# Four layers on one core: edge fills, a later large fill, paired Gelus and convolution rows loaded ahead

## The chip, the cores and the metric

The kernel runs on one core of a Trainium2 chip. The metric is the device time of one execution in microseconds (us). The core's engines work in parallel, each through its own instruction queue in order: PE (matmul), DVE or VectorE (elementwise and scans), ACT (activations), POOL or GpSimd (elementwise and transfers), SP (transfers alone).

## The reference, cut to what matters

The input x has 8 images of 384 channels and 32 x 32 pixels, in fp32. Four layers follow each other:

- Layer 0 normalizes x over the channels, multiplies by in_proj to get u and z, runs a four-tap convolution over the 1024 pixels in both directions, makes delta, B and C from it, and then a state scan: `h = exp(delta * A) * h + delta * u * B`, `y = sum over 16 states of h * C`, forwards and backwards. y times silu(z) goes through out_proj; a 3x3 depthwise convolution of the normalized image with a sigmoid is added.
- Layer 1: a 1x1 convolution (c1), a 3x3 depthwise convolution (dw), a 1x1 convolution (c2), linear attention, a layer norm and an MLP of 384 x 1536 x 384 with Gelu, with residual sums.
- Layer 2: seven depthwise convolutions of up to 13 x 13, summed; the kernel merges them into one 13x13.
- Layer 3: a 1x1 convolution, another 13x13 depthwise convolution, and Gelu.

## The kernel before, in words

The 384 channels are three chunks of 128 partitions, an image is two halves of 512 pixels. A scheduler of the tile framework sets the order on each engine from the order in which the program emits work; the order quoted in this text is that of the built program.

**Start.** The images with a border of zeros for the 3x3 convolutions (`xn_d`, `h_d`) and the padded sequence (`u_d`) lie in DRAM, two slots each. L464 to L470 fill all of them with zeros, in pieces of 384 elements per channel. `front(0)` (L599) then runs alone: the mean square through `rsqrt_mean` (L577: sums by PE, Ln and Exp on ACT, spreading by PE), the image stored by `put_image` (L554), the products of in_proj, the 3x3 convolution (`conv3`, L559, tiles lc_i and lc), the four-tap convolution (ut), deltas.

**Scan.** `scan(b)` (L720) has 48 rounds per image. In each, ACT makes da (L807, Exp), VectorE du (L812) and two pairs of scans hs (L824), POOL multiplies hs by C (L833, tile bct), and PE adds the states into acc (`sums`, L757, through `together`, L521). hs has eight buffers, two per round. Loads of dlt, vr and bct come through SP's queue. At the end of an image half zr (L780) is stored to `g_d`.

**Work beside the scan.** A planner at L1114 holds jobs: a generator, a planned cost, a first and a last round. After each round it advances the job that is furthest behind, by the cost that each `yield` reports. `front(b)` of the next image has a plan of 100, `layer1` of the image before one of 310, `fold` (which scales weights, and at L860 fills `x2_d`, the padded input of the 13x13 convolution, with zeros in three transfers of 5008 KB) one of 30. The layer 1 of the last image runs alone after the scans.

`layer1` (L901) multiplies g by out_proj (op, L914, added by VectorE at L916), runs c1 for half 1, then half 0, with one image store per half (L926), then dw (L933, copied by ACT at L934), c2 (L942), attention, the layer norm, and the MLP (L1072): for each of 12 groups of 128 hidden units, and each half, the first product mf, Gelu (L1081), and the second product mo (L1083). ACT loads another function table whenever it goes from exponentials to Gelu and back. PE's result tiles for most products are `psum` (tag mm, two buffers) and `long_psum` (tag mo, three).

**13x13 convolutions.** `conv` (L275) goes over 48 blocks of 8 channels. POOL loads a block's rows (xt, L290, four buffers), VectorE shifts copies of them (L296), SP and ACT load windows of taps (tp), PE multiplies (L308). `put2` stores through POOL; `put3` (L374) applies Gelu on ACT into ot (three buffers) and stores through POOL (L377).

Of the kernel before, what the change touches and what calls it, by code (L numbers as in the profile page):

```python
# [19 lines left out]
H = 32  # L20
# [48 lines left out]
def tile_layers(  # L69
# [190 lines left out]
    with tc.tile_pool(name="cw", bufs=1, reuse_waits="tile") as cwp, tc.tile_pool(  # L260
# [14 lines left out]
        def conv(g_d, src_d, tag, put):  # L275

            xt = tp = None
            for g in range(NQ):  # L280
                n, first = divmod(4 * g, NCH)
                if first == 0:
                    xt = cxp.tile([P, NCH, RL], FP, tag="xt", name=f"xt_{tag}_{n}", bufs=4)

                    at = [H * ((n % 2 * 2 + e) % NSH) for e in range(NSH)]
                    src = bass.AP(
                        src_d.tensor, src_d[NCH * n, 0, 0].offset,
                        [[RL, H], [H * RL, NCH], [1, RL]],
                    )
                    nc.gpsimd.dma_start(xt[at[0] : at[0] + H], src)  # L290
                    for m in range(n, min(n + 1 + N_WIN // 2, NB_C)):
                        if (tag, m) not in wins:
                            load_windows(g_d, tag, m, [nc.sync, nc.scalar])
                    tp = wins[tag, n]
                    for e in (1, 2):
                        nc.vector.tensor_copy(  # L296
                            xt[at[e] : at[e] + e * H, :, 0 : RL - e - (e - 1)],
                            xt[at[0] : at[0] + e * H, :, e : RL - (e - 1)],
                        )
                ps = cps.tile([P, HALF], FP, tag="cv", name=f"cv_{tag}_{g}")  # L300
                for t in range(KT):
                    for e in range(4):
                        c = first + e
                        row = xt[:, c, NSH * t : NSH * t + B * (W + PADW) - PADW]
                        rhs = bass.AP(
                            row.tensor, row.offset, [row.ap[0], [W + PADW, B], [1, W]]
                        )
                        nc.tensor.matmul(  # L308
                            ps[H * e : H * (e + 1), 0:BW],
                            tp[:, c, :].rearrange("p (j t) -> p j t", t=KT)[:, :, t], rhs,  # L310
                            start=(t == 0), stop=(t == KT - 1), skip_group_check=True,
                        )
                put(g, ps[:, 0:BW])
# [60 lines left out]
        def put3(g, ps):  # L374
            ot = cxp.tile([P, BW], FP, tag="ot", name=f"ot_{g}", bufs=3)
            nc.scalar.activation(ot, ps, AF.Gelu, bias=gbias[:, g : g + 1])  # L376
            nc.gpsimd.dma_start(  # L377
                ov[g * P : (g + 1) * P], ot.rearrange("p (b w) -> p b w", w=W)
            )
# [4 lines left out]
def _layers01(tc, nc, B, xv, x2_d, dram, ident, mean_w, eps5, eps6, one, half, minus1, vec, bns, bnt,  # L384
# [12 lines left out]
    with ExitStack() as ctx:  # L397
# [66 lines left out]
        for i in range(2):  # L464
            for t, n in ((xn_d, IMG), (u_d, UL), (h_d, IMG)):
                pads = t[i].rearrange("(c p) i -> p c i", p=P)
                for c in range(NC):
                    for a in range(0, n, C):
                        e = min(n, a + C)
                        nc.gpsimd.dma_start(pads[:, c, a:e], zero[:, 0 : e - a])  # L470
# [4 lines left out]
        def psum(name):  # L475
            return psp.tile([P, HALF], FP, tag="mm", name=name, bufs=2)
# [25 lines left out]
        def defer(n, fn):  # L502
            late.append([n, fn])
# [8 lines left out]
        def dense(ps, w, m, rhs):  # L512
            for k in range(NC):
                nc.tensor.matmul(  # L514
                    ps, w[:, k, m * P : (m + 1) * P], rhs[k] if isinstance(rhs, list) else rhs[:, k, :],
                    start=(k == 0), stop=(k == NC - 1),
                )

# [35 lines left out]
        def put_image(t_d, slot, h, t, queue):  # L554

            v = t_d[slot].rearrange("(c p) i -> p c i", p=P)
            queue.dma_start(v[:, :, (W + 2) + HIMG * h : (W + 2) + HIMG * (h + 1)], t)

        def conv3(t_d, slot, h, c, taps, name, psum=psum):  # L559

            ims, made = [], []
            for j in range(4):
                im = sp.tile([P, 18 * (W + 2)], FP, tag="im", name=f"{name}_i{j}", bufs=N_IM)
                src = bass.AP(
                    t_d.tensor, t_d[slot, 32 * (4 * c + j), 16 * h * (W + 2)].offset,
                    [[IMG, 32], [1, 3], [1, 18 * (W + 2) - 2]],
                )
                made.append(nc.sync.dma_start(im[:96, 0 : 18 * (W + 2) - 2], src))
                ims.append(im.rearrange("p (h w) -> p h w", w=W + 2))
            ps = psum(name)  # L570
            col32(
                ps, lambda j, i: taps[:96, (4 * c + j) * 3 + i, :],
                lambda j, i: ims[j][:96, i : i + 16, 0:W], 3, made,
            )
            return ps

        def rsqrt_mean(srcs, eps, name):  # L577
# [10 lines left out]
            nc.scalar.activation(r, r, AF.Exp, scale=-0.5)  # L588
            ps = psum(f"{name}_b")
# [9 lines left out]
        def front(b):  # L599

            xn = []
            for h in range(2):
# [7 lines left out]
                rstd = rsqrt_mean(sqs, eps6, f"ms_{b}_{h}")  # L610
# [7 lines left out]
                yield 3  # L618
# [18 lines left out]
            for h in range(2):  # L637
                for c in range(NC):
                    xr = t2(f"xr_{b}_{h}_{c}")
                    nc.sync.dma_start(xr, xv[b][:, c, bass.ts(h, HALF)])  # L640
                    ps = conv3(xn_d, b % 2, h, c, t3, f"lc_{b}_{h}_{c}")
# [14 lines left out]
            for h in range(2):  # L656
# [37 lines left out]
                for c in range(NC):  # L694
# [23 lines left out]
                    yield 3  # L718

        def scan(b):  # L720
# [65 lines left out]
            for k, (d, h, c) in enumerate(units):  # L786
                cols = bass.ts(h, HALF)
                second = k % (2 * NC) >= NC
                for r in range(NR):
# [12 lines left out]
                    for i in range(2):  # L802
# [32 lines left out]
                        ))  # L835
                        hs.append(t)
# [19 lines left out]
        def fold():  # L856

            RL = x2_d.shape[2]
            for c in range(NC):
                nc.gpsimd.dma_start(  # L860
                    x2v[c], zero[:, 0:RL].rearrange("p (o r) -> p o r", o=1).to_broadcast([P, H, RL])
                )
                yield 0
# [37 lines left out]
        def layer1(b):  # L901
# [17 lines left out]
            for h in (1, 0):  # L919
                hh, mid = image6(f"hh_{b}_{h}")  # L920
                for m in range(NC):
                    ps = long_psum(f"h_{b}_{m}_{h}")
                    dense(ps, w, m, xx[h])
                    nc.scalar.activation(mid[m], rows(ps), AF.Identity, bias=bias1[:, m, :])  # L924
                    yield 3
                put_image(h_d, b % 2, h, hh, nc.scalar)  # L926
            t3 = tapw(taps3b, f"t3b_{b}")
            dws = []
            for h in range(2):
                dw = a6(f"dw_{b}_{h}")  # L930
                dws.append(dw)
                for c in range(NC):
                    ps = conv3(h_d, b % 2, h, c, t3, f"dw_{b}_{h}_{c}", long_psum)  # L933
                    nc.scalar.copy(dw[:, c, :], ps)  # L934
                    yield 3
# [126 lines left out]
            for h in range(2):  # L1062
                xn = xns[h]
                sqs = [t2(f"vs_{b}_{h}_{k}") for k in range(NC)]
                for k in range(NC):
                    nc.scalar.activation(sqs[k], xn[:, k, :], AF.Square)
                rstd = rsqrt_mean(sqs, eps5, f"var_{b}_{h}")
                for k in range(NC):
                    nc.vector.tensor_mul(xn[:, k, :], xn[:, k, :], rstd)
                yield 3  # L1070

            for h in range(2):  # L1072
                acc = [long_psum(f"mo_{b}_{h}_{m}") for m in range(NC)]
                for i in range(FF // C):
                    wa = wtile(w1_d[:, i * C : (i + 1) * C], f"w1_{b}_{h}_{i}")
                    wb = wtile(w2[i * C : (i + 1) * C, :], f"w2_{b}_{h}_{i}")
                    for f in range(NC):
                        ps = psum(f"mf_{b}_{h}_{i}_{f}")
                        dense(ps, wa, f, xns[h])
                        hm = t2(f"hm_{b}_{h}_{i}_{f}")  # L1080
                        nc.scalar.activation(hm, ps, AF.Gelu, bias=biasf[:, NC * i + f, :])  # L1081
                        for m in range(NC):
                            nc.tensor.matmul(  # L1083
                                acc[m], wb[:, f, m * P : (m + 1) * P], hm,
                                start=(i == 0 and f == 0), stop=(i == FF // C - 1 and f == NC - 1),
                            )
                        yield 6

                def last(h=h, acc=acc):
                    for m in range(NC):  # L1090
                        o = xx[h][:, m, :]
                        nc.vector.scalar_tensor_tensor(  # L1092
                            o, acc[m], vec("mlp_b2", m), o, ALU.add, ALU.add
                        )
                        nc.gpsimd.dma_start(  # L1095
                            x2v[
                                m, :, h * (H // 2) : (h + 1) * (H // 2),
                                PADW + b * (W + PADW) : PADW + b * (W + PADW) + W,
                            ],
                            rows(o),  # L1100
                        )

                defer(0, last)
                yield 0
# [9 lines left out]
        jobs = [[fold(), 30, 0, rounds, 0], [prepare, 7, rounds, 2 * rounds, 0]]  # L1114
# [124 lines left out]
```

## Time and profile before

| | us |
|---|---|
| three runs, lowest / median / highest | 5220.93 / 5224.48 / 5226.53 |
| profiled execution, its own time | 5218.79 |
| span of that execution in the profile | 5217.0 |
| PE, VectorE, ACT, POOL busy | 4288.4, 3813.8, 2740.1, 2988.6 |
| first scan of image 0 starts, last pair of scans of image 7 starts | 216.9, 4187.9 |
| 13x13 convolutions, about | 4603 to 4822, 4958 to 5217 |

A window line gives, for a stretch, the busy time of each engine with its number of instructions, then the TensorE clock that was granted (1 is full speed), the busy share of the 16 DMA engines and what they moved in GB/s. A group line has the source line, engine, operation, result and operands, the count, then busy time and the mean of one in ns, and after the second bar the idle time of the engine before it and what ended it. A wait line reads "engine tile line <- what ended the wait: us in total, times, longest". PEld is PE's weight load.

### The profile page before, as it was taken

To read this page: it belongs to the slowest core of one execution; us is meant where nothing else is said; L and a number is where in the kernel's file an instruction comes from. 1 tells how busy PE (TensorE), PEld (TensorE's weight loads), DVE (VectorE), ACT (ScalarE), POOL (GpSimd) and SP (SyncE) were. 2 spreads that over 40 slices of the span, in tenths; PEclk is the share of its full clock that TensorE was granted. 3 is DMA by queue.
4 is the path that set the end of the run, shared out by engine and by line. 5 is a ranking of instruction groups with operands and counts; after the bars stand their busy time and mean duration, and the time that the engine had idled before them with its cause. 6 is when DMAs were issued, how large, how long until landed. Compare 5 with 4: busy or idle time off the path is not lost. (4 is left out here: it accounts for less than half of the span.)

```text
span 5217.0 us, 58464 instructions
## 1 busy us (share of the span) xinstructions
PE 4288.4 (82%) x20128; PEld 1783.5 (34%) x20128; DVE 3813.8 (73%) x3861; ACT 2740.1 (53%) x3816; POOL 2988.6 (57%) x1600
## 2 busy tenths in 40 slices
PE   4675568888988998899889888998878869968977
PEld 1121123333333333333333333333323324457456
DVE  0399899988888798879887888788978911056255
ACT  1455444785478557855775577567735712100211
POOL 3276666676667666766676657566856850033056
PEclk8676679899989998999899989999989989989989
DMA  9856447575756675767576757765653572289696
GB/s 285 243 200 213 160 150 224 194 211 171 211 202 196 180 218 181 208 177 223 172 221 182 220 177 201 202 214 168 176 166 121 158 157 67 61 181 251 204 192 139
DMA packets 545969, 975.11 MB, mean 187 GB/s; under 512 B 57049, under 2 KB 221385, under 8 KB 545673
## 3 DMA queue, kind: packets, MB, share of 16 engines
q1 hardware_dynamic: 401648, 663.89, 42.4%
q0 software_dynamic: 61408, 215.60, 16.1%
q10 hardware_dynamic: 82616, 91.90, 6.2%
q8 instruction: 159, 2.61, 0.2%
q14 instruction: 138, 1.12, 0.1%
HBM read 726.36 MB, written 244.81 MB: 186 GB/s over the span
## 5 line engine op out<-in xcount | busy, mean ns | idle before, releaser
L833 POOL TENSOR_TENSOR hs<-hs,bct 128x1024 f32<-128x1024 f32 x768 | 2411.2, 3140 | 991.2 <-DVE carry L829 473.1
L807 ACT ACTIVATE da<-dlt,neg_a 128x512 f32<-128x512 f32 x1536 | 1035.4, 715 | 774.4 <-DVE hs L824 721.2
L824 DVE TENSOR_TENSOR_SCAN hs<-da,du 128x512 f32<-128x512 f32 x768 | 902.2, 1208 | 243.0 <-ACT da L807 143.2
L812 DVE TENSOR_TENSOR du<-vr,bct 128x1024 f32<-128x1024 f32 x768 | 1059.3, 1379 | 25.4 <-DMA vr<-v_d 14.9
L824 DVE TENSOR_TENSOR_SCAN hs<-da,carry,du 128x512 f32<-128x512 f32 x768 | 944.0, 1267 | 56.9 <-PE acc L531 16.9
L531 PE MATMUL acc<-hs,selt 128*32 128x512 f32 x2304 | 560.8, 661 | 181.3 <-POOL hs L833 181.2
L1083 PE MATMUL mo<-hm,w 128*128 128x512 f32 x1152 | 572.9, 638 | 91.7 <-ACT hm L1081 91.4
L514 PE MATMUL mf<-ln,w 128*128 128x512 f32 x1152 | 564.4, 626 | 10.9 <-DMA w<-w_d 10.9
L526 PE MATMUL acc<-hs,selt 128*32 128x512 f32 x768 | 421.4, 647 | 75.6 <-POOL hs L833 50.4
L1083 PEld LDWEIGHTS mo<-hm,w 128*128 128x128 f32 x1152 | 219.6, 200 | 440.4 <-issue 243.7
L807 ACT ACT_TABLE_LOAD x278 | 356.7, 1283 | 7.5 <-ACT hh L924 2.7
L514 PEld LDWEIGHTS mf<-ln,w 128*128 128x128 f32 x1152 | 222.0, 200 | 334.7 <-issue 309.4
L514 PE MATMUL in<-xn,win 128*128 128x512 f32 x576 | 293.9, 642 | 13.2 <-ACT uz L628 8.8
L308 PE MATMUL cv_b<-xt_b,tp_b 128*32 128x256 f32 x3072 | 192.8, 404 | 68.2 <-DVE xt_b L296 36.6
L308 PE MATMUL cv_a<-xt_a,tp_a 128*32 128x256 f32 x3072 | 184.7, 390 | 55.5 <-DVE xt_a L296 31.0
L296 DVE COPY xt_b<-xt_b 32x2496 f32<-32x2496 f32 x96 | 146.0, 1521 | 109.4 <-DMA xt_b<-xp_d 103.1
L1081 ACT ACTIVATE hm<-mf,biasf 128x512 f32<-128x512 f32 x192 | 131.9, 687 | 176.2 <-PE mf L514 174.3
L1095 POOL DMA_DIRECT2D x_d<-xx x48 | 56.4, 1178 | 292.8 <-DVE xx L1092 292.7
L531 PE MATMUL dw<-dw_i,t3b 96*32 96x512 f32 x1056 | 210.3, 636 | 7.5 <-DMA dw_i<-h_d 7.2
L308 PEld LDWEIGHTS cv_b<-xt_b,tp_b 128*32 128x32 f32 x3072 | 160.4, 140 | 100.9 <-issue 74.1
L531 PEld LDWEIGHTS acc<-hs,selt 128*32 128x32 f32 x2304 | 93.0, 114 | 291.3 <-POOL hs L833 271.1
L1081 ACT ACT_TABLE_LOAD x146 | 187.3, 1283 | 2.6
(195 smaller groups left out, 5804.0 us busy)
## 6 DMA issues: line engine op xcount, KB each, us to landing
dlt<-dl_d SPq DMA_DIRECT2D x384, 256.0 KB, 4.2
vr<-v_d SPq DMA_DIRECT2D x384, 256.0 KB, 5.0
bct<-bc_d SPq DMA_DIRECT2D x256, 256.0 KB, 3.8
ut<-u_d SPq DMA_DIRECT2D x192, 257.5 KB, 5.6
lc_i<-xn_d SPq DMA_DIRECT2D x192, 228.8 KB, 5.4
dw_i<-h_d SPq DMA_DIRECT2D x192, 228.8 KB, 4.5
w<-w_d SPq DMA_DIRECT2D x64, 576.0 KB, 6.2
w<-in_w SPq DMA_DIRECT2D x64, 576.0 KB, 5.5
```

Of the source, the lines that this page charges most:

```text
L296: nc.vector.tensor_copy(xt[at[e] : at[e] + e * H, :, 0 : RL - e - (e - 1)], xt[at[0] : at[0] + e * H, :, e : RL - (e - 1)],)
L308: nc.tensor.matmul(ps[H * e : H * (e + 1), 0:BW], tp[:, c, :].rearrange("p (j t) -> p j t", t=KT)[:, :, t], rhs, start=(t == 0), stop=(t = ...
L514: nc.tensor.matmul(ps, w[:, k, m * P : (m + 1) * P], rhs[k] if isinstance(rhs, list) else rhs[:, k, :], start=(k == 0), stop=(k == NC - 1),)
L526: first = product()
L531: tc.keep_in_program_order(product())
L807: nc.scalar.activation(da[:, bass.ts(j, HALF)], dlt[:, bass.ts(j, HALF)], AF.Exp, scale=neg_a[:, g, r : r + 1],)
L812: nc.vector.tensor_mul(pairs(du), pairs(vt), bct[r][:, 0:1, :].to_broadcast([P, 2, HALF]),)
L824: nc.vector.tensor_tensor_scan(t[:, s][:, way], da[:, s][:, way], du[:, s][:, way], k_c if second else 0.0, ALU.mult, ALU.add,)
L833: made.append(nc.gpsimd.tensor_mul(pairs(t), pairs(t), bct[r][:, 1:2, :].to_broadcast([P, 2, HALF])))
L1081: nc.scalar.activation(hm, ps, AF.Gelu, bias=biasf[:, NC * i + f, :])
L1083: nc.tensor.matmul(acc[m], wb[:, f, m * P : (m + 1) * P], hm, start=(i == 0 and f == 0), stop=(i == FF // C - 1 and f == NC - 1),)
L1095: nc.gpsimd.dma_start(x2v[m, :, h * (H // 2) : (h + 1) * (H // 2), PADW + b * (W + PADW) : PADW + b * (W + PADW) + W,], rows(o),)
```

## The change

- The fills of `xn_d`, `u_d` and `h_d` cover only the first and the last elements (34 or 3 per channel), in 12 transfers; the inside is written by the image stores anyway.
- The three fills of `x2_d` in `fold` depend on the newest multiplication of POOL, report a cost of 2 each, and `fold` has a plan of 36.
- In `layer1`, c1 runs in an order that finishes chunks 0 and 1 first, each chunk is stored by itself, and the rows of a 3x3 convolution are loaded one convolution ahead (`rows3`, split from `conv3`); dw runs chunk by chunk.
- `rsqrt_mean` ends after Ln and Exp; the spreading is a function of its own, with a `yield` between.
- In the MLP, Gelus come as two together and one alone; the second products of a group are emitted after the next group's first products and Gelus, at a cost of 7 per group.
- In `conv`, loads of rows are emitted two blocks ahead, shifts one block ahead, windows before rows; ot has six buffers.

```diff
@@ conv
+            def load(n):
+                for m in range(n, min(n + 1 + N_WIN // 2, NB_C)):
+                    if (tag, m) not in wins:
+                        load_windows(g_d, tag, m, [nc.sync, nc.scalar])
...
+                nc.gpsimd.dma_start(xt[at[0] : at[0] + H], src)
+            for n in range(2):
+                load(n)
+            shift(0)
...
-                    nc.gpsimd.dma_start(xt[at[0] : at[0] + H], src)
+                    load(n + 2)
+                    if n + 1 < NB_C:
+                        shift(n + 1)
@@ put3
-            ot = cxp.tile([P, BW], FP, tag="ot", name=f"ot_{g}", bufs=3)
+            ot = cxp.tile([P, BW], FP, tag="ot", name=f"ot_{g}", bufs=6)
@@ fills
-        for i in range(2):
-            for t, n in ((xn_d, IMG), (u_d, UL), (h_d, IMG)):
+        for t, n, e in ((xn_d, IMG, W + 2), (u_d, UL, 3), (h_d, IMG, W + 2)):
+            for i in range(2):
                 pads = t[i].rearrange("(c p) i -> p c i", p=P)
-                for c in range(NC):
-                    for a in range(0, n, C):
-                        e = min(n, a + C)
-                        nc.gpsimd.dma_start(pads[:, c, a:e], zero[:, 0 : e - a])
+                for a in (0, n - e):
+                    nc.gpsimd.dma_start(
+                        pads[:, :, a : a + e],
+                        zero[:, 0 : NC * e].rearrange("p (c e) -> p c e", e=e),
+                    )
@@ fold
+                tc.add_manual_dep(fill.ins, newest[0].ins.name, behind, reason="fill")
+                yield 2
@@ front
-                rstd = rsqrt_mean(sqs, eps6, f"ms_{b}_{h}")
+                yield 0
+                r = rsqrt_mean(sqs, eps6, f"ms_{b}_{h}")
+                yield 1
+                rstd = spread_rows(r, f"ms_{b}_{h}")
@@ layer1, c1 and dw
-            for h in (1, 0):
-                hh, mid = image6(f"hh_{b}_{h}")
-                for m in range(NC):
...
-                put_image(h_d, b % 2, h, hh, nc.scalar)
+            for m, h in ((0, 1), (1, 1), (0, 0), (1, 0), (2, 1), (2, 0)):
+                if (m, h) == (2, 0):
+                    ahead = ready()
...
+                put_image(h_d, b % 2, h, hhs[h][0], nc.scalar, slice(m, m + 1))
+            while ahead:
+                c, h, loaded = ahead
+                ahead = ready() if todo else None
+                ps = conv3(loaded, c, t3, f"dw_{b}_{h}_{c}", long_psum)
@@ layer1, MLP
-                    for f in range(NC):
-                        ps = psum(f"mf_{b}_{h}_{i}_{f}")
-                        dense(ps, wa, f, xns[h])
...
-                        yield 6
+                    for fs in [(0, 1), (2,)]:
...
+                        together([
+                            partial(nc.scalar.activation, hm, ps, AF.Gelu, bias=biasf[:, NC * i + f, :])
+                            for f, hm, ps in zip(fs, hms, pss)
+                        ], [made])
+                        if behind_gelu:
+                            behind_gelu.pop()()
...
+                        behind_gelu.append(second)
+                        yield 7
@@ planner
-        jobs = [[fold(), 30, 0, rounds, 0], [prepare, 7, rounds, 2 * rounds, 0]]
+        jobs = [[fold(), 36, 0, rounds, 0], [prepare, 7, rounds, 2 * rounds, 0]]
```

## The prediction

> **What bounds the kernel now.** The page's chain of waits names only the last 8% of the span, so I cut the span into its stages and read the busy time of each engine in them. The boundaries are the first and last scan instruction of VectorE (L824), found in its groups of instructions, and the first and last matmul of each 13x13 convolution.
>
> ```profile
> core 0: us, PE busy (x) PEld busy (x) DVE busy (x) ACT busy (x) POOL busy (x), PEclk, DMA share, GB/s
> 0.00:216.00 216.00, 113.74 (x399) 35.76 (x400) 23.41 (x75) 44.38 (x62) 56.42 (x109) 0.77 0.96 277
> 216.00:715.00 499.00, 314.49 (x1085) 96.67 (x1081) 454.55 (x430) 273.18 (x380) 327.72 (x160) 0.71 0.55 186
> 715.00:3747.00 3032.00, 2657.39 (x9994) 992.77 (x9992) 2577.70 (x2583) 2005.79 (x2721) 1988.84 (x891) 0.93 0.65 196
> 3747.00:4195.00 448.00, 370.76 (x1263) 144.82 (x1262) 382.39 (x386) 247.68 (x353) 317.45 (x113) 0.90 0.50 145
> 4195.00:4603.00 408.00, 326.72 (x950) 137.69 (x952) 36.43 (x51) 68.40 (x110) 64.84 (x101) 0.90 0.46 94
> 4603.00:4822.00 219.00, 186.59 (x3090) 159.97 (x3086) 156.85 (x148) 17.86 (x48) 70.02 (x68) 0.98 1.06 239
> 4958.00:5217.00 259.00, 192.77 (x3072) 160.44 (x3072) 145.98 (x96) 45.49 (x96) 151.02 (x144) 0.93 0.79 166
> ```
>
> The start (0 to 216) is bound by transfers: the DMA share is 0.96 while no engine is half busy, but PE. Image 0 (216 to 715) runs at VectorE's pace, 455 of 499 us. Images 1 to 6 (715 to 3747) have VectorE 85% busy: 3032 - 2578 = 454 us of idle time, 76 per image. Image 7 idles 66 us more. The tail (4195 to 4603) is PE alone. The first 13x13 convolution has the DMA engines full; the second has 259 - 193 = 66 us without a matmul.
>
> What ends VectorE's idle time in images 1 to 6:
>
> ```profile
> DVE hs L824 <- ACT da L807: 133.8, 49, 10.6
> DVE hs L824 <- PE acc L531: 68.4, 25, 5.6
> DVE xx L916 <- PE op L514: 58.3, 26, 4.4
> DVE qp L1043 <- PE rzb L1042: 25.2, 20, 3.9
> DVE lg L646 <- ACT lg L643: 25.0, 23, 1.9
> DVE xx L942 <- PE c L514: 23.9, 11, 4.1
> DVE ln L1069 <- PE var_b L591: 14.0, 12, 2.5
> ```
>
> These are late arrivals in queues that run in order. VectorE waits for exponentials stuck on ACT behind a Gelu or a convolution's copy, and for hs buffers that PE has not yet summed because other products stand before the sums.
>
> **What the Trainium skill says.** "ScalarE: Activation LUTs", What ACT_TABLE_LOAD costs: about 1283 ns a load and a drain of about 1380 ns. The trace agrees on the first and shows no such drain (at 14.16 us a load starts 0.02 us after the activation before it), so I count 1283:
>
> ```profile
> L807 ACT ACT_TABLE_LOAD x278 | 356.7, 1283 | 7.5 <-ACT hh L924 2.7
> L1081 ACT ACT_TABLE_LOAD x146 | 187.3, 1283 | 2.6
> ```
>
> "DMA: Bandwidth & Descriptors", Queues, rings and completion order: each DMA engine goes round robin between its queues by packets, so a large fill slows the loads of other queues. The trace agrees: lc_i loads land in a median 15.9 us during the start and 5.4 over the kernel. Same page, Specifications: below 512 B a write is read-modify-write; the new edge fills have pieces of 136 and 12 B. The nearest row, the old 2 KB remainders of xn_d, lands in 4.9 us. "SBUF — State Buffer", SBUF: two separate sides: a fp32 VectorE copy keeps GpSimd from writing descriptors. The trace agrees: L377 takes 1146 ns beside the copies L296, the similar store L712 563 ns in the scan.
>
> **The change, part by part.**
>
> *Zero-fills (L470, L860).* Gone from the start are 66 small fills, 2 x 384 x (1156 + 1030 + 1156) x 4 B = 10.3 MB, and three large ones, 15.4 MB, that move behind the first scan rounds; 12 edge fills come, 0.2 MB. 25.7 MB at the 277 GB/s of the stage are 93 us, the ceiling. By events:
>
> ```profile
> DVE lg L646 <- ACT lg L643: 120.7, 6, 82.5
> PE lc L526 <- DMA lc_i<-xn_d: 48.5, 3, 38.6
> SPq L568 <- DMA xn_d<-xn: 24.3, 1, 24.3
> ```
>
> Now image 0's second half lands at 27.0 (issued 11.4), its products run from 33.9 to 66.4, lc from 105 to 163, the four-tap conv of the first half to 184, the scan begins at 216. Without fills the second half lands near 17 (5.6 us, like other 768 KB loads), so the products end near 57. The image is stored at about 28 and in the rows' order of SP eight lc loads now stand before the weights that wait for a buffer, so lc starts at 57. Six chunks at 5.5 us (half of a landing of 5.4, plus 2.6 us on PE, rounded up) end near 90, three more near 106; the unchanged 31 us of deltas and loads follow: scan at 137, **80 us** earlier. Bounds 50 and 93.
>
> The large fills are now issued after the multiplications of rounds 0, 2 and 5 of the built order. 15.4 MB take 15.4/277 = 56 us of the engines where their share is 0.55 to 0.75, so most fits into the free part. POOL reuses eight completion counters in turn: the eighth transfer after the first fill, a store of v, waits for its landing (31.5 us), and behind it on POOL stand the next multiplications L833, for which PE's sums wait. VectorE has eight hs buffers, four rounds of 7.8 us = 31 us, to go on. I charge **10 us**; bounds 0 and 35.
>
> *Convolution rows, c1 order, image store in chunks (L554, L559, L918 to L935).* In the before, all rows wait for a store of 816 KB (8.3 us) and their load (4.5) with ACT's copies dw (L934) in order before the exponentials. Image 3 shows a 9.6 us stop of VectorE there and 4.1 us at L942. Counted in the built order (a 128x512 product is two instructions of 0.43 us, as they follow each other in the start), PE's work between two sums falls there from 26 us to 8. Gain per image: 10 of 13.7.
>
> *Products in pairs, second product one step later (L1072 on).* Gelu groups fall from 24 to 16 an image; in the built program ACT's table loads fall from 653 to 572: 81 x 1.283 = 104 us of ACT. ACT is 66% busy, so this lies beside VectorE's work and counts only through the waits on da: 14.2 us of image 3 fall in the Gelu stretch, I take half, 7. PE no longer waits for Gelu (91.7 us, L1083 in the groups).
>
> *Costs of a step.* Layer 1's steps sum to 322 against a plan of 310 before, and to 290 after. So before, the rest of an image's MLP runs into the next image: PE has 38 us of products between two sums at the boundary, 18 after. Image 3 stops there for 7.6 us on sums and, with g loaded only after SP was free at 1750, 12.5 us on op (L916), 3 more after it: 23. The chain sum, store, load, product stays, so I leave 8: gain 15. Against it, the first MLP rounds have 34 us between two sums where before the largest was 21: up to 34 - 21 = 13 us of stop, charged 6.
>
> *Split means (L577).* var_b 2.4 and ms_b 2.4 per image: gain 3. rzb, lg, pj, zr (11.7 per image) stay.
>
> Per image 10 + 7 + 15 - 6 + 3 = 29, of 76 idle. Queues give late arrivals back elsewhere; I take 25 (bounds 8 and 36), for six images **150 us**. Image 7: op 18.7 and c 16.4 us of waits on VectorE, **25 us** (5 to 35).
>
> *Tail.* The last MLP of image 6 leaves the tail: the last sum waits on PE until 4214 although POOL's product ended at 4193, g is loaded at 4243. At 4194 the same 12 us of store and load give 4208: 35 us. dw waits 20 us (L526) between the last h product and its rows; a chunked store and one load, 13 us, started 7.7 us earlier leave 6: gain 13. Half of the former may be work already counted in image 7, so **35 us** (15 to 50). Its MLP has no PE gap over 0.9 us: nothing.
>
> *13x13 convolutions.* "Two blocks ahead" moves little: in the built order of before, POOL already issues each row load two or three blocks ahead. The 13.9 us at its start wait for xp_d and stay. Six ot buffers remove ACT's waits for the store, 41.7 us of ACT, of which 11.6 reach PE: **10 us** (-5 to 25).
>
> Sum: 80 - 10 + 150 + 25 + 35 + 10 = 290. The profiled execution took 5218.8 (span 5217.0); 5218.8 - 290 = 4929. Since the median of the runs is 5.7 above it and bounds lie lower on the gain side, I say **4940**.
>
> **Rivals.** *A, the forecast* (0.72): 4850 to 5030. *B, the scan gives its gains back* (0.21): the MLP is packed into 17 of 48 rounds with 8 to 9 us of PE each beside sums of about 1, against VectorE's 7.8; PE becomes the bound there and only start, tail and convolutions remain: 5224 - 70 - 35 - 10 = 5109, or about 5080 with a fifth of the scan's gain. For it: PE is 88% busy. Against it: that counts overlapping pieces; PE has rounds without any product after. *C, slower* (0.05): a pair holds both PSUM buffers "mm" until both Gelus are done. A Gelu group takes 1.28 + 2 x 0.69 us behind up to four exponentials of 0.715, 5.5 us, covered by the previous group's products, 2.6 us after a single. If PE, with the sums queued behind, stops VectorE 3 us in each of 16 steps of 7 images, 336 us are lost: 5270. It decides from 290 / 112 = 2.6 us a step. Against it: hs buffers absorb single stops. *D* (0.02): no effect beyond 0.2%, about what a measurement of this kernel tells from no change.
>
> **How the numbers follow.** A and B are faster, C slower. 4850 to 5100 takes in A and most of B. Faster 0.93, same 0.02, slower 0.05.
>
> **What would show it.** First scan at 125 to 150 us; VectorE idle under 60 us an image; no MLP product after the last scan; table loads x572; dw rows wait under 8 us; out waits on ACT near zero. An unchanged image period (505 us) would prove B; PE waits "mf <- ACT hm" of hundreds of us, C. A scan start after 180 would break the first step.

## The result and the profile after

The changed kernel takes 5048.59 us (5042.81 to 5056.85); the kernel before took 5225.5 us in the same set of runs. The ratio is 0.9663 (95% interval 0.9646 to 0.9680), 177 us or 3.4% faster. The prediction said 4940 us, so the direction and the range (4850 to 5100) held, and the size was too large: 285 us were forecast.

The view by stages of the changed kernel, cut where the same events fall (first scan of image 0, of image 1, of image 7, last scan, first and last product of each 13x13 convolution):

```profile
core 0: us, PE busy (x) PEld busy (x) DVE busy (x) ACT busy (x) POOL busy (x), PEclk, DMA share, GB/s
0.00:142.00 142.00, 98.66 (x404) 34.43 (x406) 23.99 (x75) 45.54 (x64) 25.19 (x52) 0.89 0.88 246
142.00:672.00 530.00, 296.62 (x1056) 93.02 (x1054) 457.45 (x432) 265.78 (x373) 330.31 (x163) 0.68 0.63 203
672.00:3638.00 2966.00, 2635.57 (x10080) 1003.75 (x10080) 2556.48 (x2589) 1923.45 (x2662) 2005.15 (x893) 0.94 0.67 202
3638.00:4066.00 428.00, 365.87 (x1266) 145.99 (x1268) 377.77 (x383) 231.79 (x339) 313.28 (x111) 0.92 0.53 153
4066.00:4433.00 367.00, 302.10 (x878) 129.67 (x874) 32.42 (x46) 64.93 (x106) 65.09 (x99) 0.88 0.45 96
4433.00:4645.00 212.00, 185.52 (x3070) 159.70 (x3072) 155.88 (x143) 17.51 (x47) 66.09 (x68) 0.98 1.07 244
4795.00:5048.00 253.00, 193.57 (x3072) 163.79 (x3072) 144.94 (x94) 45.49 (x96) 154.84 (x140) 0.94 0.79 165
```

Against the same events of before (216.9, 718.2, 3747.9, 4190.4, 4602.8 and the end at 5217.0):

| stage | before | after | gained | forecast |
|---|---|---|---|---|
| start, to the first scan | 216.9 | 142.4 | 74.5 | 80 |
| image 0 | 501.3 | 529.5 | -28.2 | -10 |
| images 1 to 6 | 3029.7 | 2966.0 | 63.7 | 150 |
| image 7 | 442.5 | 428.5 | 14.0 | 25 |
| tail | 412.4 | 366.8 | 45.6 | 35 |
| 13x13 convolutions, pointwise between | 614.2 | 614.8 | -0.6 | 10 |
| sum | 5217.0 | 5048.0 | 169.0 | 290 |

The size of the start came near the forecast. Of the 121 us that are missing, 86 lie in images 1 to 6. VectorE's waits there (ms_b and var_b are the spread mean squares of the front's norm and of layer 1's, rzb the spread reciprocals of the attention, lg the sigmoid branch of the 3x3 convolution, zr the gated output):

```profile
DVE hs L857 <- PE acc L551: 165.7, 57, 11.7
DVE qp L1087 <- PE rzb L1086: 27.8, 18, 4.4
DVE xn L644 <- PE ms_b L619: 27.7, 10, 4.5
DVE lg L677 <- ACT lg L674: 25.8, 24, 3.0
DVE xx L952 <- PE op L533: 22.5, 7, 6.3
DVE hs L857 <- ACT da L840: 12.4, 13, 1.5
```

The waits that the change was to remove are gone or shorter: da fell from 133.8 us to 12.4, op from 58.3 to 22.5, and c (23.9) left the list. In their place the waits for hs buffers that PE has not summed yet rose from 68.4 us to 165.7, with stops of up to 11.7, and ms_b from 5.4 to 27.7. I then sorted VectorE's idle gaps over 0.3 us of the six images by round (48 to an image; a round begins with every second product du, L845). Per image, in us:

| rounds | before | after | what it was, and what it is |
|---|---|---|---|
| 0 to 7 | 17.4 | 4.5 | op and sums at the boundary; op |
| 8 to 12 | 13.1 | 8.3 | da behind dw, c2; sums |
| 13 to 29 | 15.3 | 15.4 | rzb, lg, var_b; the same |
| 30 to 38 | 14.7 | 9.0 | da in the Gelu stretch; sums, dl |
| 39 to 47 | 3.0 | 18.9 | sums, ms_b; sums (round 46 has 9.3), ms_b |

The first, second and fourth line give 23.4 us an image; the last takes 16 back. What is left is 7 us, and 3 more in smaller gaps and busy time, together the 10.6 us an image of the stage table. So the question for the runs was whether the crowded end of the image is a fault beside the gains or their price.

### The profile page after: what moved, and what is told of

Same layout as the page of the kernel before. It is cut to its first block, busy times and chain, and to the rows that moved or that the text cites. A ratio compares the mean times of both kernels' runs of the same rounds, so it can differ in the third digit from the quotient of the medians.

```text
span 5048.0 us, 58439 instructions
## 1 busy us (share of the span) xinstructions
PE 4205.7 (83%) x20128; PEld 1787.7 (35%) x20128; DVE 3789.3 (75%) x3861; ACT 2632.2 (52%) x3735; POOL 2975.1 (59%) x1546
## 3 DMA queue, kind: packets, MB, share of 16 engines
q0 software_dynamic: 58048, 205.76, 15.4%
## 5 line engine op out<-in xcount | busy, mean ns | idle before, releaser
L845 DVE TENSOR_TENSOR du<-vr,bct 128x1024 f32<-128x1024 f32 x768 | 1019.2, 1327 | 46.3 <-DMA vr<-v_d 34.9
L533 PE MATMUL mf<-ln,w 128*128 128x512 f32 x1152 | 546.1, 620 | 22.8 <-DMA w<-w_d 11.7
L1166 PE MATMUL mo<-hm,w 128*128 128x512 f32 x1152 | 530.3, 599 | 13.8 <-DVE xx L1133 13.8
L546 PE MATMUL acc<-hs,selt 128*32 128x512 f32 x768 | 428.5, 653 | 74.4 <-POOL hs L866 63.7
L840 ACT ACT_TABLE_LOAD x233 | 298.9, 1283 | 9.5 <-DMA dw_i<-h_d 3.0
L326 PE MATMUL cv_b<-xt_b,tp_b 128*32 128x256 f32 x3072 | 193.6, 407 | 67.9 <-DVE xt_b L302 44.1
L533 PE MATMUL op<-g,wo 128*128 128x512 f32 x288 | 156.4, 695 | 61.3 <-DMA g<-g_d 61.3
L533 PEld LDWEIGHTS in<-xn,win 128*128 128x128 f32 x576 | 114.1, 207 | 215.2 <-issue 161.5
L326 PEld LDWEIGHTS cv_a<-xt_a,tp_a 128*32 128x32 f32 x3072 | 159.7, 138 | 74.3 <-issue 28.7
```

What stands on the lines that cost most here:

```text
L326: nc.tensor.matmul(ps[H * e : H * (e + 1), 0:BW], tp[:, c, :].rearrange("p (j t) -> p j t", t=KT)[:, :, t], rhs, start=(t == 0), stop=(t = ...
L533: product = nc.tensor.matmul(ps, w[:, k, m * P : (m + 1) * P], rhs[k] if isinstance(rhs, list) else rhs[:, k, :], start=(k == 0), stop=(k ...
L546: first = product()
L840: nc.scalar.activation(da[:, bass.ts(j, HALF)], dlt[:, bass.ts(j, HALF)], AF.Exp, scale=neg_a[:, g, r : r + 1],)
L845: nc.vector.tensor_mul(pairs(du), pairs(vt), bct[r][:, 0:1, :].to_broadcast([P, 2, HALF]),)
L1166: nc.tensor.matmul(acc[m], wb[:, f, m * P : (m + 1) * P], hm, start=(i == 0 and f == 0), stop=(i == FF // C - 1 and f == NC - 1),)
```

## The experiments

The kernels ran in three sets on three chips, on which the kernel before took 5270, 5227 and 5236 us. The first set holds e1 to e4, the second c1 and e5 to e7, the third e8 to e11 (the numbers are only names). So kernels of different sets are compared by their ratio to the kernel before on the same chip; a hundredth of that ratio is 52 us. The changed kernel is at 0.966; of the three sets it ran in the second alone. Kernels of one set are also compared by stages; where stages of different sets stand side by side, the text says so.

**Its own time again (c1).**

> The changed kernel itself, unaltered, beside the kernel before on this chip. Both theories: 0.9663 of the kernel before, as measured first; it is the base for the others.

5051.61 us, ratio 0.9656 (0.9634 to 0.9677). Its start (142.0) and tail (367.0) agree with the first profile; image 0 took 521.2 us instead of 529.5 and images 1 to 6 2976.6 instead of 2966.0, which shows how far the stages of one kernel differ.

**The start (e2, e1).** Large fill first again, plan 30:

```
-                fill = nc.gpsimd.dma_start(...)
-                tc.add_manual_dep(fill.ins, newest[0].ins.name, behind, reason="fill")
-                yield 2
+                nc.gpsimd.dma_start(...)
+                yield 0
```

> The changed kernel with the three large fills back at the start and their plan of 30, the edges alone otherwise. Theory 1 (15.4 MB at 277 GB/s are 56 us of a stage that is bound by transfers): first scan near 190 us, image 0 in about 501 us, so 5049 + 48 - 28 = 5069 us. Rival (the start has room for them beside its computing, because its products, not its transfers, set it now): first scan below 160 us, image 0 in about 501 us, 5030 us or less, faster than the changed kernel.

5168.51 us, ratio 0.9811 (0.9790 to 0.9832). And with the small fills over whole buffers as well:

> The changed kernel with all zero-fills as before: small fills over the whole buffers and the three large ones, all at the start. Theory 1 (the two stages pay for themselves: 74.5 us won at the start, 28 us lost in image 0, nothing carried on): first scan near 217 us, image 0 in about 501 us, 5049 + 46 = 5095 us (5085 to 5105). Rival (the start's gain was given back later, in a place not seen): within 10 us of 5049.

5190.29 us, ratio 0.9842 (0.9824 to 0.9860). The first scan came at 207.4 us with the large fill first and at 226.4 with all fills, against 144.3 in the kernel with single products (below), which has the changed start and ran on the same chip; image 0 took 508.9, 508.2 and 532.3 us. So there the small fills are worth 18 us up to image 1 and the large one 40: 63 us earlier, 23 lost in image 0. Both rivals fall. The ratios say more than theory 1, 96 us for the whole part where 46 were expected; 58 us of it stand in these two stages. The rest sits in images 1 to 7, the tail and the convolutions, where this part does nothing and where this chip made the kernel before slower too; the changed kernel wasn't run on it, so this rest stays open. Another order is not the reason as far as image 3 shows: there ACT, VectorE, POOL and SP run the same instructions in the same order as in the changed kernel.

These two kernels show that the moved fill costs image 0 some 23 us. Where it costs them can be looked for in the waits of POOL and VectorE, here in the changed kernel between 142 and 672 us, the last line in the kernel before between 217 and 718:

```profile
POOL v_d L744 <- DMA x_d<-zero: 14.1, 1, 14.1
```

```profile
DVE du L845 <- DMA vr<-v_d: 23.9, 3, 18.4
DVE hs L857 <- ACT da L840: 18.8, 6, 6.6
DVE zr L813 <- PE acc L551: 13.1, 4, 4.2
DVE hs L824 <- ACT da L807: 10.3, 4, 5.4
```

The first fill is issued at 154.9 and lands at 181.7. POOL's fourth store of v after it waits 14.1 us for that, as the prediction said. Other transfers pay too: VectorE waited 10.3 us for da in image 0 before and 18.8 now, and for vr loads, which were no wait before, 5.5 us besides the 18.4 that end where the first scan begins. Together these are 14 of the 28 us by which image 0 grew. Not all of the rest is the fill's: zr's wait for sums rose from 6.8 to 13.1, and it is 15.0 with the large fill first as well.

**Layer 1's rows (e5).** Image store in one piece, rows asked for where they are used:

```
+            for h in (1, 0):
+                hh, mid = image6(f"hh_{b}_{h}")
+                ...
+                put_image(h_d, b % 2, h, hh, nc.scalar)
...
-                ahead = ready() if todo else None
-                ps = conv3(loaded, c, t3, f"dw_{b}_{h}_{c}", long_psum)
+                ps = conv3(rows3(...), c, t3, f"dw_{b}_{h}_{c}", long_psum)
```

> The changed kernel with the image store in one piece, the h order and the 3x3 rows of layer 1 as before. Theory 1 (the traces before and after: VectorE's stops in rounds 8 to 12 fell from 13 us an image to 8, and the tail's 13 us): 5 x 6 + 13 = 43 us slower than the changed kernel. Rival (the part is worth the 10 us an image of the forecast): 60 + 13 = 73 us slower. Second rival (what it saves at round 9 comes back at once): within 10 us of it.

5137.37 us, ratio 0.9816 (0.9793 to 0.9839). Images 1 to 6 took 3038.0 us, 61.4 more than the changed kernel's 2976.6 in this set, or 10.2 an image; the tail 374.1 against 367.0. The rival, the forecast's 10 us an image, is right for these images; theory 1's 5, read off the gaps of the two traces, was half of it. The tail lost 7, where both had said 13. Its waits of VectorE in images 1 to 6:

```profile
DVE hs L857 <- PE acc L551: 128.4, 40, 11.9
DVE hs L857 <- ACT da L840: 85.5, 26, 12.1
```

The da wait of round 9 is back, 9.0 us an image.

**Pairs (e3).** The hidden products one at a time, the second product still one step later:

```
-                    for fs in [(0, 1), (2,)]:
+                    for fs in [(0,), (1,), (2,)]:
...
-                        yield 7
+                        yield 4 if fs[-1] == 2 else 5
```

> The changed kernel with the hidden products one at a time instead of in pairs, still with the second product one step later; costs 5, 5, 4 in place of 7, 7 per three, so the plan's total stays 290. Theory 1 (pairs help ACT: fewer table loads, fewer late exponentials): table loads rise from 572 towards 650, VectorE's waits for da return by some 5 us an image, 5049 + 35 = 5084 us. Rival (a pair makes a lump of products that stops the sums): waits of hs for acc fall by 8 us an image in the last 16 rounds, 4995 us.

5177.65 us, ratio 0.9828 (0.9807 to 0.9849). Images 1 to 6 took 3058.4 us against 3006.1 with the large fill first on the same chip, which has the pairs: 8.7 us an image. The forecast had 7. Table loads are 649, as theory 1 expected. Its rival is right about the sums, since the stops of rounds 39 to 47 fall from 21.8 us an image to 6.8, but not about the time: more comes back in other rounds. The waits, images 1 to 6:

```profile
DVE hs L857 <- ACT da L840: 129.7, 80, 4.2
DVE hs L857 <- PE acc L551: 111.7, 35, 8.9
DVE xx L952 <- PE op L533: 63.6, 10, 12.6
```

But this run does not show that the table loads are the cause. Although its costs sum to 290 as well, the last hidden products still run in round 0 of the next image (seen at image 3), where those of the changed kernel end in round 46, and op stops VectorE for 10.6 us an image where it was 7.8 with the pairs. And with cost 9 (below) the pairs stay, with 573 table loads, and VectorE waits for da just as long (129.1 us). So the 8.7 us are what this edit costs in this arrangement.

**The planner's costs (e4, then e8 to e10).** First, layer 1 as a whole at the pace of before:

```
-            jobs.append([seconds[b], 310, ...])
+            jobs.append([seconds[b], 279, ...])
```

> The changed kernel with 279 as layer 1's plan in place of 310, so that the steps' sum stands to the plan as before (290/279 = 322/310) and the end of the hidden products runs into the next image again. Theory 1 (the early end costs more in rounds 42 to 47, 16 us an image, than the clean boundary saves, 11): images 1 to 6 about 30 us shorter, but the tail 35 us longer, 5054 us. Rival (the clean boundary is worth what was forecast, 15 an image, and the stops at the end have another cause): images 1 to 6 some 60 to 90 us longer, tail 35 longer, 5145 to 5175 us.

5463.58 us, ratio 1.0368 (1.0347 to 1.0390): slower than the kernel before, and neither theory's number. The edit did more than I meant by it. It delays not the hidden products alone but all of layer 1, so that its attention stands beside other steps of the next image's front. Images 1 to 6:

```profile
DVE hs L857 <- PE acc L551: 233.5, 52, 15.9
DVE qp L1087 <- PE rzb L1086: 123.8, 6, 20.7
DVE xx L952 <- PE op L533: 76.7, 6, 17.2
DVE xn L644 <- PE ms_b L619: 75.0, 5, 16.4
DVE xx L1133 <- PE mo L1166: 60.4, 5, 12.1
```

The rzb stop, 20 us an image, now stands among the front's dt products and deltas: in image 3 ACT loads six function tables within it, 1283 ns each. The right test changes the cost of a pair step alone, 7 in the changed kernel, so that the attention stays in its rounds:

```
-                        yield 7
+                        yield 9      (then 8, then 6)
```

> The changed kernel with 9 instead of 7 as the planner's cost of a pair step, so that layer 1's steps sum to 322 against 310 as before, its attention stays in its rounds, and only the hidden products stretch over the image boundary again. Theory 2 (pairs and rows gave what was forecast, 18 us an image; the early end of the hidden products took 8 back, by the stops of rounds 42 to 47): images 1 to 6 shorter than the changed kernel's by 30 to 50 us, the tail longer by 35, the whole 5035 to 5055 us. Rival (the forecast's own step: the clean boundary is worth 15 an image less 6): images 1 to 6 longer by 54 us, tail by 35, the whole 5140 us.

> The changed kernel with 8 as the cost of a pair step: steps sum to 306 against 310, so the hidden products fill the image to its last round and hardly pass it. Theory 2: the stops of rounds 42 to 47 fall by half or more and the boundary stays nearly clean, images 1 to 6 shorter by 50 us, 5000 us. Rival (the front's products of rounds 42 to 47 collide with the hidden ones wherever those end): within 15 us of the changed kernel, or slower.

> The changed kernel with 6 as the cost of a pair step: steps sum to 274 against 310, so the hidden products end near round 42, ahead of the front's norm and input products of rounds 42 to 47. Theory 2 (the stops at the end are a collision of the two): they go, but rounds 29 to 42 get 1.17 times the products each; if PE has the room, 5000 us; Rival (PE is full in those rounds): stops of hs for acc rise there by 10 us an image or more, 5070 to 5110 us.

| cost of a pair step | layer 1's sum, against 310 | us | ratio (interval) | images 1 to 6 | tail |
|---|---|---|---|---|---|
| 9 | 322 | 5232.08 | 0.9994 (0.9980 to 1.0008) | 3114.5 | 390.7 |
| 8 | 306 | 5235.50 | 1.0002 (0.9992 to 1.0011) | 3119.0 | 384.3 |
| 7 (changed kernel, second set) | 290 | 5051.61 | 0.9656 (0.9634 to 0.9677) | 2976.6 | 367.0 |
| 6 | 274 | 5111.09 | 0.9764 (0.9750 to 0.9779) | 3019.9 | 375.3 |

Theory 2, that the early end of the hidden products takes 8 us an image back, is refuted: with cost 9 the whole gain of 3.4% is gone. Images 1 to 6 lose 138 us, 23 an image; the rival had said 54 in all. Cost 8 falls on its rival's side ("or slower"), cost 6 at the slow end of its rival's range. The chip is not the cause: e11, which ran beside these with cost 7, took 2980.3 us for the same images. Nor is the clock, which was 0.92 of full speed there against 0.94: PE's work in them took 2647 us with cost 9 and 2640 in the changed kernel. The waits of cost 9, images 1 to 6:

```profile
DVE hs L857 <- ACT da L840: 129.1, 54, 4.8
DVE hs L857 <- PE acc L551: 124.0, 47, 8.9
DVE xx L952 <- PE op L533: 70.3, 11, 13.2
DVE xn L644 <- PE ms_b L619: 33.2, 5, 7.7
DVE xx L1133 <- PE mo L1166: 31.4, 5, 9.1
```

of cost 8, the same stage:

```profile
DVE hs L857 <- PE acc L551: 190.4, 51, 11.4
DVE hs L857 <- ACT da L840: 89.6, 50, 4.0
DVE du L845 <- DMA vr<-v_d: 72.7, 7, 13.1
DVE xx L952 <- PE op L533: 48.4, 11, 9.4
```

and of cost 6:

```profile
DVE hs L857 <- PE acc L551: 105.9, 37, 8.3
DVE xx L1133 <- PE mo L1166: 38.3, 10, 5.3
DVE zr L813 <- PE acc L551: 30.0, 12, 4.2
```

At 9, op and the da waits of before have both come back. At 8 they have in part, and a load of vr that comes late in round 40 takes 10.8 us an image besides. At 6 the stop of round 46 is gone, as theory 2 said, but sums and mo stop VectorE by 17 us an image in rounds 36 and 37, which had 4.4. None of the costs that I tried is faster than 7.

One thing that goes with a late end is when SP asks for g, the first thing that the next image's layer 1 needs. Its line at the boundary of images 3 and 4, before, after, with cost 9 and with cost 8:

```profile
L909 SPq DMA_DIRECT2D g<-g_d x1: 533/533/533, 2261.6 to 2261.6; - x1
```

```profile
L945 SPq DMA_DIRECT2D g<-g_d x1: 377/377/377, 2172.7 to 2172.7; - x1
```

```profile
L945 SPq DMA_DIRECT2D g<-g_d x1: 365/365/365, 2265.8 to 2265.8; - x1
```

```profile
L945 SPq DMA_DIRECT2D g<-g_d x1: 381/381/381, 2265.9 to 2265.9; - x1
```

The first scan of image 4 starts at 2233.2, 2157.7, 2220.8 and 2233.4 us, so g is asked for 28, 15, 45 and 33 us into the image. With single products it is 36 and with cost 6 it is 3. A sum below the plan is thus no promise: with cost 8, seen at image 3, the last hidden products run in rounds 0 and 1 of the next image too. The planner gives the later steps their rounds whether g was late or not. In the boundary of images 2 and 3, PE's op products run in round 4 of before, rounds 0 to 3 of the changed kernel, 2 to 4 with cost 9 and 1 to 4 with single products; dw is in rounds 9 to 12, 6 to 10, 7 to 10 and 7 to 10. Where op is late, op, h and dw are pressed together, and I take this for a part of the loss. Round 10 has 4.7 us of stops an image with cost 9 and round 9 has 6.8, where the changed kernel has 4.4 and 1.9. But lateness alone does not order the kernels: cost 6 asks earliest and is slower than 7, and with cost 8 g is asked for earlier than with cost 9 and with single products, but images 1 to 6 take longest. Why one unit of cost is worth so much is not shown by these runs.

**The stop of round 46 (e7).** In image 3 of the changed kernel PE waits 4.5 us until 2130.1 for win, the first weights of the next front, with the sums queued behind. SP issues this load at 2125.2, behind a bct load that waits for POOL. So I asked for it at the beginning of the front:

```
             xn = []
+            wins_b = [wtile(inproj_t[:, 0:C], f"win_{b}_0")] if b else []
...
-                w = wtile(inproj_t[:, e * C : (e + 1) * C], f"win_{b}_{e}")
+                w = wins_b.pop() if wins_b else wtile(...)
```

> The changed kernel, but each image's first input-projection weights are asked for at the beginning of the front instead of after its norm, so that their load stands ahead of the bct loads of round 46. Theory 1 (VectorE's 9.3 us at round 46 are this load: in SP's queue behind bct loads that wait for POOL, with PE's sums queued behind the product that needs it): 6 x 8 = 48 us faster than the changed kernel. Rival (PE is too full in the last rounds anyway, or the early load takes a weight buffer from the hidden products): within 15 us of it, or slower.

5045.75 us, ratio 0.9656 (0.9636 to 0.9675), the same as the changed kernel in its set: the rival is right. Round 46 fell from 9.5 to 5.9 us an image and round 45 rose from 0.7 to 2.9. The queue of products stays. Images 1 to 6:

```profile
DVE hs L858 <- PE acc L551: 154.5, 56, 8.5
```

**Split means (e11).** Mean and spreading in one step again:

```
-            r0 = rsqrt_mean(sq, eps5, f"var_{b}_0")
-            sq = squares(1)
-            yield 1
...
+            for h in range(2):
+                scaled(h, rsqrt_mean(squares(h), eps5, f"var_{b}_{h}"))
+                yield 3
```

> The changed kernel with the means and their spreading in one step again, in the front and in layer 1, with the same costs. Forecast's step: 3 us an image lost, 18 us slower. Theory 2 (VectorE's waits at var_b fell from 2.3 to 1.6 us an image and those at ms_b rose from 0.9 to 4.6, so the split is no gain): within 10 us of the changed kernel.

5076.14 us, ratio 0.9692 (0.9678 to 0.9707). That is 0.36% above the changed kernel's 0.9656, with an interval of about 0.26% on that difference and another chip: 19 us, give or take 14, where the forecast's step had said 18. The stages say less: images 1 to 6 took 2980.3 us, 3.7 more than in the second set, and 6 each of image 0 and the convolutions are as large as the spread between profiles of these stages. I call it inconclusive; 3 us an image is not what images 1 to 6 show.

**Convolutions (e6).** Rows loaded by program order in their own block, three ot buffers:

```
-            ot = cxp.tile([P, BW], FP, tag="ot", name=f"ot_{g}", bufs=6)
+            ot = cxp.tile([P, BW], FP, tag="ot", name=f"ot_{g}", bufs=3)
...
-                    load(n + 2)
-                    if n + 1 < NB_C:
-                        shift(n + 1)
+                    nc.gpsimd.dma_start(xt[at[0] : at[0] + H], src)
```

> The changed kernel with both 13x13 convolutions as before: rows loaded in the block that needs them by program order, three ot buffers. Theory 1 (the two stages took 614.8 us after and 614.2 before; ACT's waits for stores went, and PE waits for rows in their place): within 5 us of the changed kernel. Rival (the two edits cancel: one gains 10, one loses 10): also 5 us, but then the waits of the 13x13 stage for rows fall below 37 us.

5058.21 us, ratio 0.9670 (0.9654 to 0.9686), not apart from the changed kernel. PE's waits of the second convolution, changed kernel of the same set (c1):

```profile
PE cv_b L326 <- DVE xt_b L302: 27.9, 4, 13.8
PE cv_b L326 <- issue: 25.8, 16, 3.1
PE cv_b L326 <- ACT ot L394: 13.6, 13, 1.3
```

and with the old convolutions:

```profile
PE cv_b L308 <- DVE xt_b L296: 38.5, 7, 14.0
PE cv_b L308 <- issue: 17.4, 11, 3.0
PE cv_b L308 <- ACT ot L376: 12.4, 8, 3.8
```

With three buffers ACT waits 41.8 us for the output stores, as before the change; with six that wait is gone. PE's waits for ot are 12.4 and 13.6 us, so six buffers took nothing from them; I read them as waits for ACT's Gelu and not for a free buffer. Its waits for rows and for its sequencer tell nothing about the order of the loads: they are 27.9 and 25.8 here, and 44.1 and 12.5 in the first profile of the same changed kernel. So theory 1's exchange of one wait for another is not shown, nor the rival's.

## Why the prediction was right in sign and range, and too large

- **Start, 80 us, measured 74.5.** Right in size, and in part by luck. The first scan came at 142.4 (137 forecast), but its first step failed: without the old fills image 0's second half was to land near 17 and its products to end near 57. It landed after 16.3 us as against 15.6 before, and they ended at 66.9. So lc began at 66.8 instead of 57. It ended at 97.8 instead of 106, and what follows took 45 us instead of 31: three errors that nearly cancel. The term put at nothing was the twelve edge fills. They move 0.44 MB (the prediction's 0.2 is a slip: 384 channels x 71 elements x 4 B x 4), and each took 5.7 to 15.8 us to land where the row that the prediction called nearest had 4.9. From 10 to 20 us the DMA engines were as busy as before, at fewer GB/s, the kernel before first:

```profile
10.00:20.00 10.00, 3.74 (x32) 2.38 (x32) 2.20 (x4) 5.69 (x9) 3.38 (x7) 1.00 1.05 152
10.00:20.00 10.00, 3.74 (x32) 2.39 (x32) 2.09 (x4) 5.80 (x9) 4.93 (x8) 1.00 1.04 130
```

No run leaves the edge fills out, so that they delay the image is likely and not shown.
- **Large fill in the scan, 10 us, measured 28** against the kernel before, 23 between two kernels of one chip (17 to 26 over the profiles of the second and third set, against 501.3 in the kernel before). Mis-sized, inside its bound of 35. I priced POOL's one wait, which came with 14.1 us. What failed is the reasoning that most of 56 us of transfers fits into the free share of the DMA engines: image 0's loads of vr, and the da that wait for loads, came later while the fill ran.
- **Images 1 to 6, 150 us, measured 63.7.** This is the step that failed. It summed 10 (rows), 7 (Gelu pairs), 15 (boundary), -6 (dense products) and 3 (split means). By the gaps the boundary gave 12.9 and the Gelu stretch 5.7, which is near; rows gave 4.8, though they cost 10.2 when taken out. *The -6 failed.* I charged one stop where the hidden products begin; the measured cost is 16 us an image where they end, in rounds 39 to 47, in waits for sums and ms_b. That the front's norm and first input products stand in the same rounds is a part of it: with cost 6, where the hidden products end earlier, the stop of round 46 is gone. It isn't the whole: with cost 9 both stand there too, less dense, and these rounds lose 8.4 us instead of 18.9.
- **And the terms do not add.** Taken out of the finished kernel one at a time, rows cost 10.2 us an image, pairs 8.7, the pair step's cost 23; the whole change brought 10.6. Rows and pairs do not pay by themselves: with cost 9 they are all there, the kernel is where it was before, and images 1 to 6 take 3114.5 us where the first profile of before, on another chip, had 3029.7. Summing edits as if each acted on the kernel before, then taking 25 for 29, allowed for late arrivals but not for this.
- **Image 7, 25 us, measured 14.** The wait for op fell from 18.7 to 4.3 us and that for c from 16.4 to nothing that is listed; sums rose from 6.7 to 19.3. Here too the gain was given back in waits for sums.
- **Tail, 35 us, measured 45.6.** Right in its mechanism. Image 6's last mo product starts at 4050 us, before the last scan at 4065 (before: 4213.8, after it). The op wait on g went from 20.1 to 15.5 us, that before dw from 20.0 to 11.0. The halving for double counting was not needed in full.
- **Convolutions, 10 us, measured nothing.** ACT's wait for the stores was not what PE waited for.
- **Rivals.** B named the right place, PE in the rounds of the hidden products, but made it the bound of the image, with nothing left but start, tail and convolutions. The image period fell from 505 to 494 us, so A happened at a little under half its size there. The whole, 5049 us, lies between the two: above A's 5030 and below B's 5080. C did not appear: PE's waits of mf for hm are 10.0 us in seven images.
- **The signs.** First scan within 125 to 150, no product of image 6 after the last scan, table loads x572 and no ACT waits for out: all came. Two did not: VectorE was to be idle for less than 60 us an image, and 2966 - 2556 = 410 us are 68; and the rows of dw were to wait under 8 us, and PE waited 11.0 before them in the tail.

"ScalarE: Activation LUTs", What ACT_TABLE_LOAD costs, held for the load itself, 1283 ns again:

```profile
L840 ACT ACT_TABLE_LOAD x233 | 298.9, 1283 | 9.5 <-DMA dw_i<-h_d 3.0 <-DVE hs L857 2.5
L546 ACT ACT_TABLE_LOAD x113 | 145.0, 1283 | 3.8 <-ACT uz L659 1.9
```

## What to carry to other kernels

When several engines share one hand-planned order, cost the arrangement and not its edits: ask for each stretch of rounds what will stand there after the whole change, above all at the seam between two images, where one job's end meets the next one's start. A wait that disappears from the list is not time won until the list's new first line is read; here da fell by 121 us and acc rose by 97. A sum that comes out near is no proof of its terms, as the start shows. And before a planner's figure is believed, move it both ways: one unit of a step's cost was worth 1% in one direction and the whole change in the other.

## What I had not expected of the hardware

That the DMA engines' free share (0.55 in image 0 before) did not carry 15.4 MB for nothing was new to me: the fills landed in 26.7 to 33.7 us each, and image 0 grew by 28 us. Nor did I expect that twelve edge fills of 0.44 MB in all would take up to 15.8 us each to land, nearly as long as the half image beside them. And the same kernel before took 5227 us on one chip and 5270 on another, more than several of the effects measured here, so runs from different chips can be set side by side only as ratios.
